# Reordering the first pass of a two-layer graph network with routed experts: the mean-square product ahead of the transposes, the scales ahead of an older block's places

## The chip, the cores and the metric

The kernel runs on one core of one Trainium2 chip. Its metric is the time of one launch on the device in microseconds (us); the time before is the median of three runs. Five engines work side by side, each through its own instructions in the order in which they were written: TensorE (PE in the profile, PEld for its weight loads), VectorE (DVE), ScalarE (ACT), GpSimd (POOL) and SyncE (SP). [...]

## The reference, cut to what matters

The input is 8192 tokens of 256 numbers, 64 to a graph. Two layers follow each other, each a graph part and a mixture of experts. Only the first half of layer 0 is touched here:

```python
xn  = layernorm(x)
agg = epsilon * xn + adj @ xn                     # per graph of 64 tokens
h   = agg @ W1 + b1                               # 256 -> 1024
h   = silu(h * rsqrt(mean(h * h) + 1e-6) * rms_w) # mean over the 1024
x1  = x + h @ W2 + b2                             # 1024 -> 256
xn1 = layernorm(x1)
logits = xn1 @ gate_w.T                           # 64 experts, the best 6 are taken
... the 6 experts' 256x256 matrices, weighted by the softmax of the 6 logits,
... then layer 1: another graph part and 8 experts, the best 2 taken
```

## The kernel before

TensorE works in fp32 here, but for the counting and bias products. The kernel goes through the program in stages: a first pass over 32 blocks of 256 tokens (the graph part of layer 0, and routing), pages of 128 rows through the 64 experts, a second pass over the 32 blocks, and pages through the 8 experts of layer 1. The routing sends each token's row six times to a table in HBM, to the place that its expert's counter gives; each of the 12 sends of a block is an indirect DMA that GpSimd issues.

The first pass is software-pipelined. Step `s` runs the stages below in this order, each for block `s - lag`; since each engine keeps the program's order, this list is also the order on every engine.

```python
staggered(NB, (
    (3, choose),                             # DVE: best 6 of the logits in pg
    (2, residual_a),                         # DVE: x1 = po + x, statistics
    (-2, load), (-1, norm_a),                # DVE: statistics of x
    (0, hidden 0), (0, hidden 1),            # PE: h; ACT: Square of each part
    (2, residual_s), (-1, norm_s),           # ACT: Ln, Exp of the variances
    (-1, norm_e), (3, weigh),                # DVE; ACT: Exp
    (0, hidden 2), (0, hidden 3),            # PE; ACT: Square
    (3, count),                              # PE: into the PSUM tile route
    (2, residual_b), (-1, norm_b),           # DVE; ACT: six copies of xn1 into xs
    (0, split_late),
    (1, project first tile, parts 0-3),      # PE
    (0, square_sum),                         # DVE: three adds
    (-1, aggregate),                         # PE; ACT: copy aggT <- ps
    (-1, load_late),
    (1, project first tile, parts 4-7),      # PE
    (2, turn),                               # PE: 4 transposes; ACT: copy xn1T <- ps
    (0, rms),                                # PE: 1 product; ACT: Ln, Exp, table load
    (3, place),                              # DVE: normalize, books, places; GpSimd: sends
    (1, project second tile),                # PE
    (2, gate),                               # PE: logits
    (0, scale),                              # DVE: 8 scales; ACT: 8 Silu, table load
    (1, load_lattice),
))
```

The stages that the change moves (cut):

```python
def hidden(b, j):                            # four tiles ph in PSUM for the four j
    B["ph", j] = ph = ph_pool.tile([P, 2, C], F32, name="ph")
    ...                                      # 4 products; then ACT:
    for c in range(2):
        nc.scalar.activation(sq[:, 2*j+c, :], ph[:, c, :], AF.Square, bias=..., scale=1.0)

def square_sum(b):                           # 8 parts -> 4 -> 2 -> 1
    h = KH
    while h > 1:
        h //= 2
        nc.vector.tensor_add(sq[:, :h, :], sq[:, :h, :], sq[:, h:2 * h, :])

def rms(b):
    nc.tensor.matmul(rms_b, lhsT=mean, rhs=sq[:, 0, :], start=True, stop=True)
    blocks[b]["rms"] = ops.rstd(rms_b, 1e-6, ...)          # ACT: Ln, then Exp
    nc.scalar.preload_act_table_set("silu_and_others")

def turn(b):
    pt = psum.tile([P, KD, C], F32, name="ps")             # pool ps: 2 buffers
    ops.transpose(pt, B["xs"][:, :, 0, :])
    nc.scalar.copy(xn1T, pt)

def scale(b):                                # reads ph, so it also frees ph
    for c in range(KH):
        nc.vector.scalar_tensor_tensor(hT[:, c, :], B["ph", c // 2][:, c % 2, :],
                                       b1[:, c:c + 1], B["rms"], op0=ALU.add, op1=ALU.mult)
        nc.scalar.activation(hT[:, c, :], hT[:, c, :], AF.Silu, scale=rms_w[:, c:c + 1])
    nc.scalar.preload_act_table_set("natural_log_exp_and_others")

def place(b):
    r0.normalize(*B["w"], B["xs"])                         # DVE: 3 small instructions
    r0.send(r0.places(b, B["hot"]), B["xs"])               # GpSimd: 12 indirect DMAs
    ...

def places(self, b, hot):                                  # of the router
    if self.J > 1 and b >= self.epoch and b % self.epoch < 3:     # epoch is 4
        (self.move_on, self.grow, self.note)[b % self.epoch]()    # DVE: 7, 10 or 6
    ...                                                    # DVE: 9 more, the last the rows
```

In three blocks of four, one of `move_on`, `grow` and `note` keeps the router's books: which expert needs a further stretch of the table.

Of the kernel before, what the change touches and what calls it, by code (L numbers as in the profile page):

```python
# [78 lines left out]
class Router:  # L79
# [199 lines left out]
    def normalize(self, w, den, xs):  # L279
# [2 lines left out]
        nc.vector.reciprocal(den, den)  # L282
        nc.vector.tensor_mul(xs[:, :, :, D + 1], w, den.unsqueeze(2).to_broadcast([P, T, K]))

    def places(self, b, hot):

        nc, T, E, K, n = self.nc, self.T, self.E, self.K, self.name
        if self.J > 1 and b >= self.epoch and b % self.epoch < 3:
            (self.move_on, self.grow, self.note)[b % self.epoch]()
        pos, cnt = self.psum[:, 0], self.psum[:, 1]  # L290
        run = self.run
        self.run = self.counts.tile([P, T, E], F32, name=n + "run")
        nc.vector.tensor_add(run[:, 1, :], run[:, 0, :], cnt[:, 0, :])
        nc.vector.tensor_add(self.run[:, 0, :], run[:, 1, :], cnt[:, 1, :])
        place = self.work.tile([P, T, E], F32, name=n + "place", bufs=1)
        nc.vector.tensor_add(place, pos, run)
        if self.J > 1:
            over = self.work.tile([P, T, E], F32, name=n + "over", bufs=1)
            nc.vector.tensor_tensor(over, place, self.end.unsqueeze(1).to_broadcast([P, T, E]), op=ALU.is_ge)
            nc.vector.tensor_mul(over, over, self.delta.unsqueeze(1).to_broadcast([P, T, E]))  # L300
            nc.vector.tensor_add(place, place, over)
        prod = self.work.tile([P, T, K, E], F32, name=n + "prod", bufs=1)
        nc.vector.tensor_mul(prod, hot, place.unsqueeze(2).to_broadcast([P, T, K, E]))
        row = self.small.tile([P, T, K], F32, name=n + "rowf")
        nc.vector.tensor_reduce(row, prod, op=ALU.add, axis=AX.X)
        out = self.small.tile([P, T, K], I32, name=n + "row")
        nc.vector.tensor_copy(out, row)
        return out
# [166 lines left out]
def two_layer_gnn_moe_kernel(ctx: ExitStack, tc: tile.TileContext, a: dict, out: bass.AP):  # L475
# [83 lines left out]
    r0 = Router(tc, const, small, dram, N, D, E0, K0, T, P, 14 * P, 4, "r0", 3)  # L559
# [23 lines left out]
    with tc.tile_pool(name="c0", bufs=1) as c0, \  # L583
# [9 lines left out]
        blocks = [dict() for _ in range(NB)]  # L593
# [96 lines left out]
        def project(b, t, lo, hi):  # L690
            B = blocks[b]
            if t == 0 and lo == 0:
                B["po"] = psum.tile([P, T, D], F32, name="ps")
                nc.tensor.matmul(B["po"], lhsT=r0.ones, rhs=late["L0_gnn_b2"], start=True, stop=False)
            for c in range(lo, hi):
                nc.tensor.matmul(B["po"][:, t, :], lhsT=B["hT"][:, c, ts(t, P)], rhs=w2[:, c, :],  # L696
                                 start=False, stop=(t == T - 1 and c == KH - 1))
# [44 lines left out]
        def count(b):  # L742
            r0.count(blocks[b]["hot"])

        def place(b):
            B = blocks[b]
            r0.normalize(*B["w"], B["xs"])
            r0.send(r0.places(b, B["hot"]), B["xs"])
            if b == READY - 1:
                r0.look_back()  # L750
            if b == 20:
                r0.look(EARLY)

        def load_lattice(b):
# [26 lines left out]
            (-1, aggregate),  # L781
            (-1, load_late),
            (1, lambda b: project(b, 0, 4, KH)),
            (2, turn),
            (0, rms),
            (3, place),
            (1, lambda b: project(b, 1, 0, KH)),
            (2, gate),
            (0, scale),
            (1, load_lattice),  # L790
        ))
        r0.page_table(sq.rearrange("p c n -> p (c n)"))
# [119 lines left out]
    with tc.tile_pool(name="c3", bufs=1, reuse_waits="tile") as c3, \  # L912
# [17 lines left out]
        blocks = [dict() for _ in range(NB)]  # L930
# [298 lines left out]
```

## Time and profile before

| | us |
|---|---|
| median of 3 runs | 2074.68 (2069.03 to 2075.51) |
| span of the profiled execution | 2434.4 |
| PE busy in it | 2043.7 (84%) |
| DVE busy | 1184.6 (49%) |
| POOL busy | 1144.3 (47%) |
| ACT busy | 1009.9 (41%) |

The profiled execution is longer than the timed ones. Its first pass lasts from the start to about 800 us; the transposes and products of the first expert pages follow from 806 us on. In a line of the timeline the columns are start and busy time in us, engine, source line, operation, operands, how many were merged, and, in brackets, how long the engine had been idle before it and who released it. TensorE's fp32 products appear as two records each, except for the transposes.

For reading the timeline: L663 is a product of `hidden` and L666 its Square, L673 `square_sum`, L677 the product of `rms`, L58 and L59 its Ln and Exp (and those of other stages), L76 the transposes of `turn` and L725 their copy, L656 the copy of `aggregate`, L685 the scales and L687 the Silu, L281 to L283 `normalize`, L226 to L259 the books, L293 to L307 `places`, L204 and L205 `choose`, L715 the six copies into `xs`, L314 the sends.

### The profile page before, as it was taken

The page shows a single profiled execution, that of the slowest core. Times are in us where ns is not written, and L with a number is a line of the kernel's source. Part 1 is how long each engine was busy: PE and PEld are TensorE (multiplying, and loading weights), DVE is VectorE, ACT ScalarE, POOL GpSimd, SP SyncE. Part 2 cuts the span into 40 slices and gives each one's busy share as a digit, 9 for nine tenths or more (in the row PEclk, how much of TensorE's full clock was granted, in tenths as well). Part 3 has the DMA queues.
Part 4 walks back from the last instruction along what each step waited for, and adds up shares of the span by engine and source line. Part 5 has one row for each costly group of instructions (what it writes and reads, how often), then busy time and mean ns, then how long its engine had stood idle before and what let it go on. Part 6 is the DMA issues. An engine that isn't in the chain of part 4 may idle for free. (4 is left out here: it accounts for less than half of the span.)

```text
span 2434.4 us, 36827 instructions
## 1 busy us (share of the span) xinstructions
PE 2043.7 (84%) x10516; PEld 1750.1 (72%) x10516; DVE 1184.6 (49%) x3981; ACT 1009.9 (41%) x2033; POOL 1144.3 (47%) x1134
## 2 busy tenths in 40 slices
PE   7887878878876578778787877888988899999997
PEld 6776767767665467666666765777777788888886
DVE  5677657667765622222222224777778422222221
ACT  5765656656655112111111212555555333333332
POOL 0345444554555656666666661233333444444443
PEclk9999889989898689889999888999999899999998
DMA  3223333433234678765555526887774476666665
GB/s 109 91 99 113 125 118 106 131 122 119 101 108 157 196 234 234 218 181 176 174 170 174 160 80 242 289 267 239 248 235 138 128 181 162 162 159 165 160 167 101
DMA packets 282557, 397.88 MB, mean 163 GB/s; under 512 B 56025, under 2 KB 236393, under 8 KB 282353
## 3 DMA queue, kind: packets, MB, share of 16 engines
q1 hardware_dynamic: 202880, 246.61, 34.5%
q0 software_dynamic: 64416, 136.14, 18.8%
q10 hardware_dynamic: 15056, 12.69, 1.6%
q8 instruction: 94, 1.54, 0.3%
q14 instruction: 111, 0.90, 0.1%
HBM read 222.84 MB, written 176.64 MB: 164 GB/s over the span
## 5 line engine op out<-in xcount | busy, mean ns | idle before, releaser
L314 POOL DMA_INDIRECT r0x<-xs,r0row x384 | 385.6, 1004 | 442.3 <-issue 343.3
L883 PE MATMUL py<-lat,pxT 128*128 x1616 | 427.9, 412 | 114.2 <-ACT pxT L870 86.0
L321 POOL DMA_INDIRECT r0y<-px x404 | 392.3, 971 | 230.9 <-DVE px L887 107.2
L883 PEld LDWEIGHTS py<-lat,pxT 128*128 128x128 f32 x1616 | 317.2, 207 | 169.7 <-ACT pxT L870 97.9
L887 DVE TENSOR_SCALAR px<-py,px 128x256 f32<-128x256 f32 x404 | 170.9, 478 | 453.2 <-PE py L883 160.9
L331 POOL DMA_INDIRECT out_x<-py_s,px x138 | 214.6, 1555 | 294.3 <-DMA out_x<-py_s,px 136.8
L870 ACT COPY pxT<-pt 128x512 f32<-128x512 f32 x202 | 113.9, 588 | 515.3 <-remote 161.9
L696 PE MATMUL ps<-lat 128*128 128x256 f32 x1024 | 267.2, 412 | 15.6 <-issue 14.4
L1167 ACT ACTIVATE phid<-ph,pw 128x256 f32<-128x256 f32 x276 | 130.9, 474 | 322.6 <-issue 211.3
L663 PE MATMUL ph<-lat 128*128 128x256 f32 x1024 | 243.8, 396 | 20.6 <-issue 14.3
L1165 PE MATMUL ph<-pxT,pw 128*128 128x256 f32 x1104 | 251.1, 381 | 0.7 <-ACT pxT L1156 0.7
L696 PEld LDWEIGHTS ps<-lat 128*128 128x128 f32 x1024 | 213.1, 211 | 53.5 <-issue 17.9
L1185 PE MATMUL py<-fw,phid 128*128 (+1 forms) x1104 | 249.7, 379 | 0.0
L663 PEld LDWEIGHTS ph<-lat 128*128 128x128 f32 x1024 | 201.1, 199 | 53.6 <-issue 19.4
L1165 PEld LDWEIGHTS ph<-pxT,pw 128*128 128x128 f32 x1104 | 210.7, 191 | 29.9 <-ACT pxT L1156 1.1
L1185 PEld LDWEIGHTS py<-fw,phid 128*128 128x128 f32 x1104 | 204.5, 190 | 25.0
L314 POOL DMA_INDIRECT r1x<-xs,r1row x128 | 126.2, 986 | 202.1 <-DVE bn_rs L1004 114.2
L666 ACT ACTIVATE lat<-ph,c_L_gnn_b 128x256 f32<-128x256 f32 x256 | 102.5, 471 | 113.1 <-remote 52.9
L868 PE MATMUL pt<-ident,px 128*128 128x128 f32 x808 | 132.3, 285 | 7.7 <-issue 7.6
L868 PEld LDWEIGHTS pt<-ident,px 128*128 128x128 f32 x808 | 107.7, 149 | 33.9 <-issue 14.0
L685 DVE SCALAR_TENSOR_TENSOR lat<-ph,c_L_gnn_b,rms 128x256 f32<-128x256 f32 x256 | 103.1, 475 | 52.3 <-ACT rms L59 45.7
L1188 DVE TENSOR_TENSOR py_s<-py,pb 128x512 f32<-128x512 f32 x69 | 47.8, 692 | 155.4 <-PE py L1185 155.4
(303 smaller groups left out, 2872.1 us busy)
## 6 DMA issues: line engine op xcount, KB each, us to landing
px<-r0x SPq DMA_DIRECT2D x404, 129.0 KB
y<-r0y SPq DMA_DIRECT2D x64, 768.0 KB
pw<-in_L_ffn_W1b SPq DMA_DIRECT2D x69, 514.0 KB
px<-r1x SPq DMA_DIRECT2D x69, 258.0 KB
x<-x SPq DMA_DIRECT2D x64, 256.0 KB
pb<-in_L_ffn_b SPq DMA_DIRECT2D x69, 128.0 KB
r0x<-r0filler ACTq DMA_DIRECT2D x64, 129.0 KB
lat<-in_x SPq DMA_DIRECT2D x32, 256.0 KB
```

What stands on the lines that cost most here:

```text
L314: i = self.nc.gpsimd.indirect_dma_start(out=self.table[:, :], out_offset=bass.IndirectOffsetOnAxis(ap=row[:, t, k:k + 1], axis=0), in_=xs[ ...
L321: d = self.nc.gpsimd.indirect_dma_start(out=self.answer[:, :], out_offset=bass.IndirectOffsetOnAxis(ap=x[:, self.D:self.D + 1].bitcast(I32 ...
L331: i, d = f"{self.name}add{i}", self.nc.gpsimd.indirect_dma_start(out=self.total[:, :], out_offset=bass.IndirectOffsetOnAxis(ap=x[:, self.D ...
L663: nc.tensor.matmul(ph[:, c, :], lhsT=w1[:, k, ts(2 * j + c, P)], rhs=B["aggT"][:, k, :], start=(k == 0), stop=(k == KD - 1))
L696: nc.tensor.matmul(B["po"][:, t, :], lhsT=B["hT"][:, c, ts(t, P)], rhs=w2[:, c, :], start=False, stop=(t == T - 1 and c == KH - 1))
L868: nc.tensor.transpose(pt[:, k, ts(q, P)], Q["px"][:, q, ts(k, P)], ident)
L870: nc.scalar.copy(xT[:, :, :n * P], pt[:, :, :n * P])
L883: nc.tensor.matmul(py[:, q, :], lhsT=xT[:, k, ts(q, P)], rhs=lat[:, ds(regs["e"][(2 * j + q) % 4], 1), k, :].rearrange("p o d -> p (o d)") ...
L887: nc.vector.tensor_scalar(px[:, q, :D], py[:, q, :], px[:, q, D + 1:D + 2], None, op0=ALU.mult)
L1165: nc.tensor.matmul(ph, lhsT=w[:, k * F1 + c * P:k * F1 + (c + 1) * P], rhs=Q["xT"][:, k, :], start=(k == 0), stop=(k == KD - 1))
L1167: nc.scalar.activation(hid[:, c, :], ph, AF.Relu, bias=w[:, KD * F1 + c:KD * F1 + c + 1], scale=1.0)
L1185: nc.tensor.matmul(py[:, t, :], lhsT=Q["hid"][:, c, ts(t, P)], rhs=fw2[:, ds(e, 1), c, :].rearrange("p o d -> p (o d)"), start=(c == 0), s ...
```

## The change

Three things are moved; nothing is added or taken out. The product of the mean squares (`rms`, with its Ln, Exp and table load) goes ahead of the transposes (`turn`, with its copy). `place` is split: its bookkeeping (`normalize` and the router's `books`) keeps its place ahead of the scales, and the rest (`places` and the sends) comes after them. The purpose is that the scales of the current block, which free the PSUM tiles of `hidden` and feed the Silu, need not stand behind the places of a block three steps older.

```diff
-    def places(self, b, hot):
-
-        nc, T, E, K, n = self.nc, self.T, self.E, self.K, self.name
+    def books(self, b):
+
         if self.J > 1 and b >= self.epoch and b % self.epoch < 3:
             (self.move_on, self.grow, self.note)[b % self.epoch]()
+
+    def places(self, b, hot):
+
+        nc, T, E, K, n = self.nc, self.T, self.E, self.K, self.name
         pos, cnt = self.psum[:, 0], self.psum[:, 1]
 ...
+        def books(b):
+            B = blocks[b]
+            r0.normalize(*B["w"], B["xs"])
+            r0.books(b)
+
         def place(b):
             B = blocks[b]
-            r0.normalize(*B["w"], B["xs"])
             r0.send(r0.places(b, B["hot"]), B["xs"])
 ...
             (1, lambda b: project(b, 0, 4, KH)),
+            (0, rms),
             (2, turn),
-            (0, rms),
+            (3, books),
+            (0, scale),
             (3, place),
             (1, lambda b: project(b, 1, 0, KH)),
             (2, gate),
-            (0, scale),
             (1, load_lattice),
```

## The prediction

> **What bounds the kernel now.** I read the page first. Its span is 2434.4 us, but the timed runs take 2074.68, so 360 us of this profile are not in the time that counts. The list of waits within the first pass (100 to 750 us, 26 or 27 steps) tells which idle time may belong to the tracing and which to the kernel:
>
> ```profile
> PE ps L76 <- ACT lat L656: 77.5, 23, 6.8
> ACT lat L656 <- remote: 58.5, 12, 6.0
> ACT lat L666 <- remote: 52.9, 12, 7.0
> DVE lat L685 <- ACT rms L59: 40.4, 9, 8.3
> DVE lat L673 <- issue: 15.7, 13, 5.0
> PE ph L663 <- DVE lat L685: 3.6, 6, 0.9
> ```
>
> ScalarE stands still some 5 us at a time (58.5 / 12), about once a step, at its copy of `aggregate` or at a Square, and no engine of this core is named. TensorE's waits at the transposes (77.5 us) and most of VectorE's waits for `rms` (up to 8.3 us) follow these stops. A step with such a stop takes 23.5 to 26.5 us. I choose to hold the stops for a cost of tracing: 26 x 5 to 7 us is 130 to 180 us, a plausible share of the missing 360. What a change does to them will then not show in the timed runs. So I work out the step from a stretch without a stop, the timelines of VectorE, ScalarE and TensorE between 514 and 536 us:
>
> ```profile
> 514.52 2.41 DVE L673 TENSOR_TENSOR lat<-lat 128x1024 f32<-128x1024 f32 x3 [0.82 <-ACT lat L666]
> 516.85 0.16 DVE L281 TENSOR_REDUCE r0den<-r0w 128x2 f32<-128x12 f32 x1
> 517.33 0.22 DVE L253 SCALAR_TENSOR_TENSOR r0cum<-r0alloc,r0cum 128x64 f32<-128x64 f32 x1
> 519.31 0.22 DVE L293 TENSOR_TENSOR r0run<-r0run,route 128x64 f32<-128x64 f32 x1
> 523.06 3.22 DVE L685 SCALAR_TENSOR_TENSOR lat<-ph,c_L_gnn_b,rms 128x256 f32<-128x256 f32 x8
> 526.21 0.23 DVE L204 MAX8 r0top<-rms_p 128x8 f32<-128x64 f32 x1
> 533.55 1.95 DVE L673 TENSOR_TENSOR lat<-lat 128x1024 f32<-128x1024 f32 x2 [0.91 <-issue]
> ```
>
> ```profile
> 518.83 0.59 ACT L725 COPY xn1T<-ps 128x512 f32<-128x512 f32 x1 [0.75 <-PE ps L76]
> 519.31 0.48 ACT L58 ACTIVATE rms<-rms_p,eps 128x256 f32<-128x256 f32 x1
> 519.82 0.42 ACT L59 ACTIVATE rms<-rms 128x256 f32<-128x256 f32 x1
> 520.25 1.28 ACT L679 ACT_TABLE_LOAD   x1
> 523.58 3.30 ACT L687 ACTIVATE lat<-lat,c_L_gnn_rms_weight 128x256 f32<-128x256 f32 x8 [2.04 <-DVE lat L685]
> 531.97 1.55 ACT L666 ACTIVATE lat<-ph,c_L_gnn_b 128x256 f32<-128x256 f32 x4
> 533.39 3.23 ACT L715 ACTIVATE xs<-x,bn_nm,rstd 128x1536 f32<-128x1536 f32 x2
> ```
>
> ```profile
> 518.19 0.60 PE L76 MATMUL ps<-ident,xs 128*128 128x128 f32 x4
> 518.62 0.60 PE L677 MATMUL rms_p<-lat,mean 128*128 128x256 f32 x2
> 523.99 7.17 PE L663 MATMUL ph<-lat 128*128 128x256 f32 x32 [0.47 <-DVE lat L685]
> ```
>
> The reader is to see that Exp ended at 520.24 and the scales began at 523.06: 2.8 us in which `rms` was ready and VectorE was still at the places; and that TensorE then waited 0.47 us at `hidden` for the first scales. That is what the change aims at. But VectorE was not idle in these 2.8 us. From start to start, in order, its step is: scales 3.15 (526.21 - 523.06); `choose` to the end of `norm_b` 6.42 (to 532.63); idle 0.92, as it waits for the last Squares; `square_sum` 2.33; `normalize` 0.48; books 1.98 (519.31 - 517.33, here `note`); places 3.75 (523.06 - 519.31). For the other blocks the same timeline has `grow` at 2.38 (287.44 to 289.82) and `move_on` at 1.45 (seven starts, 755.16 to 756.6). So VectorE's loop is 17.05 us plus 0, 1.45, 2.38, 1.98 of books: 17.05, 18.50, 19.43, 19.03, on the mean 18.50. TensorE's own step at full clock, start to start: hidden 7.0, count and bias 0.9, project 1.73, aggregate 0.89, project 1.73, transposes 0.44, rms 0.44, project 3.45, gate 0.84, together 17.4. As a check, the step of 16.46 us after 739.51, which has no aggregate, fits 17.4 - 0.9. So without stops VectorE's loop is the bound, by about 1 us a step, and TensorE's wait at `hidden` is how that shows.
>
> **What the Trainium skill says.** TensorE: Matmul & The Clock Gate, the table at its head: ScalarE, VectorE and GpSimd have a strict first-in first-out queue of 8. So an instruction that waits holds up all behind it, and only the order matters. The trace agrees: Silu waits 2.04 us behind scales that wait behind places. The same page, "What's actually happening": the clock goes to half after an idle window of about 3.4 us. The trace shows it: the mean clock is 0.86 to 0.93 in the first pass with its 5 us stops, and a timed run without the stops should have nearly full clock. ScalarE: Activation LUTs, "Table sets: the hidden batching unit": copy is in every set, so the copy of `turn` behind the load of the Silu set needs no further load; "What ACT_TABLE_LOAD costs": about 1283 ns for the load, and the trace has 1.28 us. It also adds 1380 ns of drain, which the trace doesn't show: Exp ends at 520.24 and the load starts at 520.25.
>
> **The change part by part.** No instruction is added or removed; I count from the start of the scales, X.
>
> VectorE: after the scales (3.15) now come the places (3.75), then `choose` to `norm_b` (6.42). All that hangs on them on ScalarE comes 3.75 us later. The idle 0.92 stays, since it is the way VectorE, variances on ScalarE, Squares, VectorE, all in order. `square_sum` thus starts at X + 14.24 and its result is there at X + 16.65 (2.41). Then two things run side by side. VectorE does normalize and books: X + 14.24 + 2.33 + 0.48 + books = X + 17.05, 18.50, 19.43 or 19.03. TensorE does the product: about 0.1 for the semaphore, 0.65 from its start to Ln (270.25 to 270.93 in another step), so X + 17.4. But ScalarE has not come so far: its last four Squares began at 531.97, 8.91 after X, now 12.66; then 1.42 to the copies into xs (533.39), 3.11 for those, 0.5 for the copy of `aggregate`: Ln at X + 17.69. Ln to Exp 0.51, Exp to scale 0.45: the next scales can't start before X + 18.65. So the loop becomes the larger of both: 18.65, 18.65, 19.43, 19.03, mean 18.94, where it was 17.05 (TensorE's 17.4 at best), 18.50, 19.43, 19.03. Before the change the places filled this time: `rms` was ready at about X + 16.4, before VectorE's 17.05.
>
> Over four steps that is + 1.25 to 1.6 + 0.15, or 0.35 to 0.44 a step. Books begin with block 4 at step 7, places end their share at step 31, so 25 to 28 steps: + 9 to 12 us. If the timed TensorE is slower than 17.4, it hides part of it; at 18.7 a step the difference is 0.25, + 7 us. What TensorE wins at `hidden` (0.47 to 0.86 us in a step without a stop) it will spend at `rms`, waiting for `square_sum`: off the path.
>
> The end of the pass: GpSimd's sends take 12 x (0.97 + 0.30) = 15.3 us a block, less than a step, so it has no backlog until the last step with scales (31). Block 28's places then end 3.2 us later (scales in front), and four blocks of sends, 61 us, follow one behind the other, because the steps after it are shorter than 15.3. The expert pages wait for the last send, so up to + 3.2 us, less if the page table ends later.
>
> The copy of `turn` comes 2.2 us later on ScalarE (0.51 + 0.43 + 1.28), but the second half of project, 3.45 us, lies before its reader: free.
>
> Sum: + 7 to 12 for the loop, 0 to 3 for the end, and some chance that I overrate VectorE's loop: + 7, or 2082 us.
>
> **The rivals.** First, TensorE is the bound and its wait at `hidden` is lost time: 25 x 0.5 to 0.85 us is 12 to 21 us to win, 2054 to 2062. For it: the wait is there in nearly all steps that no stop precedes, named with its releaser. Against it: TensorE's 17.4 is under VectorE's 18.5. Second, the stops are real in timed runs too. Then after each stop `rms` no longer stands behind the transposes, Ln starts about 2 us sooner (copy at 492.18, Ln at 494.82, against 492.8), and TensorE saves the 0.5 to 1.06 us of the product after the stop: about 10 to 20 us to win, 2055 to 2065. Against it: 2434 against 2075. Third, VectorE is faster untraced, below 17.4: then nothing but the end is left, 2075 to 2078. Fourth, the later sends hold up a buffer: `xs` has 3, a block's sends end about X + 6.9 + 15.3 + 2 = 24 and its buffer is written again after X + 33; no wait.
>
> **Range and chances.** My own path gives 2080 to 2090, the third 2075 to 2078, the first two about 2055 to 2065 with a fifth of the weight. So 2082, and 2062 to 2097 should hold it 8 times in 10. 2% are 41 us, 1.6 us in each of 26 steps; no path reaches that: faster 0.03, slower 0.03, same 0.94.
>
> **What would show it.** In the profile after: no waits of `hidden` for scales; a new wait of VectorE's scales for Exp (L59's place), 1 to 1.6 us in the steps without books, in steps without a stop; a wait of TensorE's `rms` for `square_sum`; Ln right behind the copy of `aggregate`. Where stops fall, the profile's span may even be shorter while the timed run is not. I am wrong if the timed run is more than 10 us faster: then VectorE's loop was not the bound. I am wrong upward beyond 20 us if a further table load or a wait of the sends shows.

## The result and the profile after

| | before | after |
|---|---|---|
| median | 2075.1 us (4 runs) | 2094.11 us (4 runs) |
| ratio | | 1.0098, 95% interval 1.0079 to 1.0117 |
| span of a profile | 2073.1 us | 2092.2 us |

The change costs 19 us. The page of before that the prediction read shows 2434 us; the profile of 2073.1 us is that of the run `control` below, the same program. All lines "of before" in this part are from it.

First the list of waits between 100 and 550 us, of before and then of after; the columns are who waited for whom, us in total, times, and the longest.

```profile
PE ps L76 <- ACT lat L656: 11.8, 16, 1.0
PE ph L663 <- DVE lat L685: 8.4, 12, 0.9
DVE lat L673 <- ACT lat L666: 22.7, 24, 1.2
```

```profile
PE rms_p L680 <- DVE r0den L281: 11.7, 19, 0.9
PE ps L76 <- ACT lat L659: 8.6, 23, 0.4
PE rms_p L680 <- DVE lat L676: 2.9, 5, 0.8
DVE lat L676 <- ACT lat L669: 22.1, 24, 1.0
DVE lat L688 <- ACT rms L59: 10.5, 7, 1.5
```

The stops of ScalarE that the prediction read are in neither. TensorE's 8.4 us at `hidden` are gone, as the change meant, and 14.6 us at `rms` are in their place (11.7 + 2.9; `r0den` is the small instruction right behind `square_sum`, which is what the product reads and so its true releaser). VectorE's wait for the last Squares is as before, some 0.92 us a step. The last line is the new one: VectorE's scales wait for Exp, 1.5 us in each of the 7 steps in which the router has no books to keep.

One such step, block 14, in the timelines of before. The upper four lines are VectorE's, the next three ScalarE's:

```profile
262.42 3.22 DVE L685 SCALAR_TENSOR_TENSOR lat<-ph,c_L_gnn_b,rms 128x256 f32<-128x256 f32 x8
...
272.91 2.41 DVE L673 TENSOR_TENSOR lat<-lat 128x1024 f32<-128x1024 f32 x3 [0.92 <-ACT lat L666]
275.71 0.21 DVE L293 TENSOR_TENSOR r0run<-r0run,route 128x64 f32<-128x64 f32 x1
279.46 0.87 DVE L685 SCALAR_TENSOR_TENSOR lat<-ph,c_L_gnn_b,rms 128x256 f32<-128x256 f32 x2
...
275.87 0.59 ACT L656 COPY lat<-ps 128x512 f32<-128x512 f32 x1
277.69 0.48 ACT L58 ACTIVATE rms<-rms_p,eps 128x256 f32<-128x256 f32 x1
278.20 0.42 ACT L59 ACTIVATE rms<-rms 128x256 f32<-128x256 f32 x1
```

and of after, with TensorE's product below:

```profile
281.55 2.41 DVE L676 TENSOR_TENSOR lat<-lat 128x1024 f32<-128x1024 f32 x3 [0.94 <-ACT lat L669]
284.27 0.18 DVE L283 TENSOR_TENSOR xs<-r0w,r0den 128x12 f32<-128x12 f32 x1
285.96 3.23 DVE L688 SCALAR_TENSOR_TENSOR lat<-ph,c_L_gnn_b,rms 128x256 f32<-128x256 f32 x8 [1.51 <-ACT rms L59]
289.10 0.21 DVE L296 TENSOR_TENSOR r0run<-r0run,route 128x64 f32<-128x64 f32 x1
...
284.51 0.59 ACT L659 COPY lat<-ps 128x512 f32<-128x512 f32 x1
284.97 0.50 ACT L58 ACTIVATE rms<-rms_p,eps 128x256 f32<-128x256 f32 x1
285.51 0.42 ACT L59 ACTIVATE rms<-rms 128x256 f32<-128x256 f32 x1
...
284.11 0.67 PE L680 MATMUL rms_p<-lat,mean 128*128 128x256 f32 x2 [0.77 <-DVE lat L676]
```

Before, from the start of `square_sum` to the scales, VectorE has 6.55 us of unbroken work (279.46 - 272.91), and Exp is done at 278.62, in its midst: nobody waits. After, `square_sum` and `normalize` end near 284.45, the places are no longer there to fill the time, and VectorE stands still until Exp ends at 285.93. The places follow at 289.10, in full. So the scales are 2.1 us nearer to `square_sum` (4.41 against 6.55), but VectorE's whole round is longer by this wait, and VectorE's round is what sets the step.

The length of a step, from one product of the mean squares to the next in TensorE's timeline, tells the same for all four kinds of block (one value of each kind, steps 18, 19, 16 and 17; the columns on the right are the experiments below):

| books of the block | before | after | `scales_alone` | `place_behind` | `half_places_2` | `books_early` |
|---|---|---|---|---|---|---|
| none | 17.35 | 18.62 | 20.00 | 19.11 | 18.00 | 17.36 |
| move_on | 18.25 | 18.66 | 20.00 | 20.59 | 17.39 | 17.35 |
| grow | 19.42 | 19.41 | 20.00 | 21.52 | 19.30 | 17.91 |
| note | 19.07 | 19.11 | 20.00 | 21.16 | 18.96 | 18.10 |
| first to last product, us | 564.4 | 579.6 | 610.0 | 621.3 | 562.4 | 545.1 |

Of the 19 us, 15.2 are thus in the loop, and the rest of the span, after the last product, went from 1482.4 to 1486.5 us: 4.1 at the end of the pass and behind it (the first product comes 0.2 us sooner).

### The profile page after: what moved, and what is told of

Read it like the earlier page. It is cut to its first block, busy times and chain, and to the rows that moved or that the text cites. A ratio compares the mean times of both kernels' runs of the same rounds, so it can differ in the third digit from the quotient of the medians.

```text
span 2092.2 us, 36857 instructions
## 1 busy us (share of the span) xinstructions
PE 1940.8 (93%) x10516; PEld 1673.9 (80%) x10516; DVE 1188.0 (57%) x3981; ACT 1015.1 (49%) x2033; POOL 1141.3 (55%) x1134
## 5 line engine op out<-in xcount | busy, mean ns | idle before, releaser
L317 POOL DMA_INDIRECT r0x<-xs,r0row x384 | 379.4, 988 | 292.9 <-issue 151.7
L891 PE MATMUL py<-lat,pxT 128*128 x1616 | 388.6, 384 | 17.9 <-ACT pxT L878 13.8
L895 DVE TENSOR_SCALAR px<-py,px 128x256 f32<-128x256 f32 x404 | 177.0, 480 | 309.9 <-PE py L891 306.2
L891 PEld LDWEIGHTS py<-lat,pxT 128*128 128x128 f32 x1616 | 293.5, 192 | 57.8 <-ACT pxT L878 17.9
L699 PE MATMUL ps<-lat 128*128 128x256 f32 x1024 | 237.7, 381 | 0.0
L666 PE MATMUL ph<-lat 128*128 128x256 f32 x1024 | 232.2, 386 | 2.7 <-DVE lat L688 2.0
L666 PEld LDWEIGHTS ph<-lat 128*128 128x128 f32 x1024 | 195.2, 193 | 29.4 <-issue 2.4
L699 PEld LDWEIGHTS ps<-lat 128*128 128x128 f32 x1024 | 190.9, 191 | 23.1
L317 POOL DMA_INDIRECT r1x<-xs,r1row x128 | 130.0, 1015 | 71.9 <-issue 22.7
L1187 DVE TENSOR_SCALAR p<-p 128x2 f32<-128x2 f32 x69 | 11.7, 169 | 226.7 <-ACT p L1186 226.7
L876 PEld LDWEIGHTS pt<-ident,px 128*128 128x128 f32 x808 | 101.2, 143 | 39.6 <-DMA px<-r0x 9.6
```

Of the source, the lines that this page charges most:

```text
L317: i = self.nc.gpsimd.indirect_dma_start(out=self.table[:, :], out_offset=bass.IndirectOffsetOnAxis(ap=row[:, t, k:k + 1], axis=0), in_=xs[ ...
L666: nc.tensor.matmul(ph[:, c, :], lhsT=w1[:, k, ts(2 * j + c, P)], rhs=B["aggT"][:, k, :], start=(k == 0), stop=(k == KD - 1))
L876: nc.tensor.transpose(pt[:, k, ts(q, P)], Q["px"][:, q, ts(k, P)], ident)
L891: nc.tensor.matmul(py[:, q, :], lhsT=xT[:, k, ts(q, P)], rhs=lat[:, ds(regs["e"][(2 * j + q) % 4], 1), k, :].rearrange("p o d -> p (o d)") ...
L895: nc.vector.tensor_scalar(px[:, q, :D], py[:, q, :], px[:, q, D + 1:D + 2], None, op0=ALU.mult)
```

## The experiments

The theory: VectorE's round sets the step in before; the change takes away the work that lay beside rms on its way through TensorE and ScalarE, so that in steps with few books a wait joins the round. The rivals: TensorE's new wait or the later copy of `turn`; the end of the pass (later sends); any delay of what comes behind the scales.

**The same program again.** No edit.

> The kernel before, with nothing changed, for a profile that holds no stops of ScalarE. VectorE's loop as the bound: 2072 to 2078 us; steps of the first pass 17.4 (no books), 18.5 (move_on), 19.4 (grow) and 19.0 us (note), with TensorE waiting at hidden for the scales and no wait of VectorE's scales for Exp. TensorE as the bound (rival): 17.4 to 17.9 in all four kinds of step. If the stops are there again in a profile whose time is near 2075, they belong to the kernel and my reading of them was wrong.

2075.11 us, ratio 1.0002 (0.9992 to 1.0013). The steps are 17.35, 18.25, 19.42 and 19.07, and scales start 17.04 us after the last ones in a step without books (262.42 to 279.46), where the sum was 17.05. VectorE's round is the bound in before.

**The product alone ahead of the transposes.**

```diff
-            (2, turn),
             (0, rms),
+            (2, turn),
```

> Only the product of the mean squares goes ahead of the transposes; places stay whole and ahead of the scales. VectorE's loop as the bound: rms was ready before the places ended and is only ready earlier now, so nothing changes: within 3 us of before. If the rival holds and the loss of the change lies in TensorE's new wait at rms or in the later copy of turn, this kernel shows the loss: 2085 to 2095.

2077.04 us, ratio 1.0005 (0.9994 to 1.0015); first to last product 564.4 us as before. This half of the change costs nothing by itself, and neither does the later copy of `turn`, which is in it too.

**The scales alone ahead of the places.**

```diff
             (2, turn),
             (0, rms),
-            (3, place),
+            (3, books), (0, scale), (3, place),
 ...
-            (0, scale),
```

> Only the scales go ahead of the places (books in front); the product stays behind the transposes. My theory, the way through ScalarE's queue: Ln now stands behind the copies into xs, the copy of aggregate, the transposes and the copy of turn, at X + 12.66 + 4.53 + 1.83 = X + 19.0, and the scales at X + 20.0 in every kind of step (19.4 and 19.0 before at most, 18.9 on the mean in the changed kernel): 25 to 28 us more than the changed kernel, some 2115 to 2122. Rival, that only the end of the pass (later sends) costs: the same as the changed kernel, 2092 to 2096.

2125.26 us, ratio 1.0239 (1.0222 to 1.0256), 3 us over the range. From step 3 on nearly every step takes 20.0 us, whatever the books (the longest is 20.9). ScalarE's queue in one of these steps:

```profile
313.26 3.23 ACT L718 ACTIVATE xs<-x,bn_nm,rstd 128x1536 f32<-128x1536 f32 x2
316.38 0.59 ACT L659 COPY lat<-ps 128x512 f32<-128x512 f32 x1
317.72 0.59 ACT L728 COPY xn1T<-ps 128x512 f32<-128x512 f32 x1 [0.75 <-PE ps L76]
318.20 0.48 ACT L58 ACTIVATE rms<-rms_p,eps 128x256 f32<-128x256 f32 x1
318.71 0.42 ACT L59 ACTIVATE rms<-rms 128x256 f32<-128x256 f32 x1
```

Ln stands behind the copy of `turn`, which waits for the transposes, which wait for the buffer that the copy of `aggregate` frees. So it begins at 318.20, though `square_sum` had ended at 315.83 (313.42 + 2.41). With the scales in front, the product has to go ahead of the transposes too: that half wins back 31 us (2125 to 2094).

**All of place behind the scales, the books too.**

```diff
-            (3, books),
             (0, scale),
+            (3, books),
             (3, place),
```

> The changed kernel with the whole of place behind the scales, normalize and the books too. If what counts is that nothing of VectorE's work lies beside the wait for rms, the 0.48 us of normalize and the books (0, 1.45, 2.38, 1.98) are added in full: steps of 19.1, 20.6, 21.5, 21.1 us against 18.65, 18.66, 19.4, 19.05 in the changed kernel; 10 x 0.5 + 6 x (1.9 + 2.1 + 2.1) = 41 us, and about 2 at the end: 2132 to 2140. Rival, that the books are hidden behind other work anyway: within 5 us of the changed kernel, 2090 to 2098.

2137.89 us, ratio 1.0296 (1.0273 to 1.0318); the steps 19.1, 20.6, 21.5 and 21.2 are the expected ones. What stands behind the scales is added in full, since VectorE now waits for Exp in every step:

```profile
301.37 3.23 DVE L688 SCALAR_TENSOR_TENSOR lat<-ph,c_L_gnn_b,rms 128x256 f32<-128x256 f32 x8 [2.00 <-ACT rms L59]
304.51 0.15 DVE L281 TENSOR_REDUCE r0den<-r0w 128x2 f32<-128x12 f32 x1
...
320.51 3.23 DVE L688 SCALAR_TENSOR_TENSOR lat<-ph,c_L_gnn_b,rms 128x256 f32<-128x256 f32 x8 [2.00 <-ACT rms L59]
```

Keeping the books in front was worth 44 us to the change.

**The old order in steps without books.** The scales stay behind the places where no books would cover rms, and in all steps before 7.

```diff
-            (0, scale),
+            (0, lambda b: scale(b) if b >= 7 and (b - 3) % 4 < 3 else None),
             (3, place),
+            (0, lambda b: None if b >= 7 and (b - 3) % 4 < 3 else scale(b)),
```

> The changed kernel, but in the steps without books (and all before step 7) the scales stay behind the places, so that no wait of VectorE for Exp is left. My sum says that the loop's loss sits in the steps whose books are too short to cover rms: the loop comes back to that of before (35.6 us for the pair of steps without books and with move_on, as before), and only the end of the pass, some 4 us, is left: 2077 to 2082. If the loss were TensorE's wait at rms or the later copy of turn, in all steps alike, a third of it would go: 2086 to 2090.

2084.35 us, ratio 1.0042 (1.0025 to 1.0059): outside both ranges, half of the loss. First to last product takes 569.8 us, 5.4 more than before; the steps are 18.0, 18.4, 19.4 and 19.1. The end of the pass takes its share too: the last send comes 70.5 us behind the last product of the mean squares, in before 67.0. In the loop a changed step after an old one doesn't return as much as I had reckoned. TensorE and VectorE around step 18, which is in the old order, and step 19, with move_on, in the new:

```profile
352.81 0.67 PE L680 MATMUL rms_p<-lat,mean 128*128 128x256 f32 x2 [0.72 <-DVE r0den L281]
353.83 0.66 PE L76 MATMUL ps<-ident,xs 128*128 128x128 f32 x4 [0.35 <-ACT lat L659]
370.81 0.59 PE L680 MATMUL rms_p<-lat,mean 128*128 128x256 f32 x2
...
372.39 3.23 DVE L688 SCALAR_TENSOR_TENSOR lat<-ph,c_L_gnn_b,rms 128x256 f32<-128x256 f32 x8 [0.71 <-ACT rms L59]
```

In step 18 TensorE waits 0.72 us for `square_sum` and then 0.35 for the copy of `aggregate`; the rest of its round is without a gap, and its next product comes after 18.0 us, where 17.35 would do. So Ln and Exp of step 19 come late, and its scales wait for them, 0.71 us here and 0.7 to 0.8 in most such steps. Here TensorE's lateness does reach VectorE.

**Half of the places back in front.** The six instructions up to the place of each row (1.7 us) go with the books; product with `hot`, sum, cast and sends stay behind the scales.

```diff
 def books(b):
     ...
     r0.normalize(*B["w"], B["xs"])
     r0.books(b)
+    B["place"] = r0.places(b, B["hot"])      # the first six instructions
 def place(b):
-    r0.send(r0.places(b, B["hot"]), B["xs"])
+    r0.send(r0.rows(B["hot"], B["place"]), B["xs"])
```

> The changed kernel with the first six instructions of places (1.7 us, up to the place of each row) back ahead of the scales with the books; only the product with hot, the sum and the cast (2.06 us) and the sends stay behind. If the loss is only that VectorE has too little to do while rms is made, it is covered now: VectorE is busy 2.33 + 0.48 + 1.69 = 4.5 us after square_sum begins, before rms is ready at 4.1, and ScalarE reaches Ln 1.7 us sooner. The steps come back to 17.4, 18.2, 19.4, 19.05 as before; with a little at the end 2074 to 2080. Rival, that any work behind the scales delays the Squares and so the loop: half of the loss stays, 2084 to 2087.

2452.52 us where before took 2438.39 on the same chip, ratio 1.007 (1.0039 to 1.0101). On this chip the kernel before takes 17% longer, with stops as in the page that the prediction read. What part of the 14 us is the change's stays open, as the changed kernel was not timed there. The second trial is on a chip on which before takes 2075.7 us:

> The same kernel as half_places, which ran on a chip on which the kernel before takes 2438 us; again on another. As there: if the loss is only that VectorE has too little to do while rms is made, 2074 to 2080 where before takes 2075; rival, that any work behind the scales delays the loop, 2084 to 2087. If before takes some 2438 again, only the ratio counts: 1.000 to 1.003 or 1.005 and more.

2074.9 us, ratio 0.9994 (0.9983 to 1.0005). The loss is gone, though 2.06 us of work and the sends still stand behind the scales. The list of waits between 100 and 550 us:

```profile
PE rms_p L685 <- DVE r0den L281: 7.9, 11, 0.9
PE rms_p L685 <- DVE lat L681: 0.8, 1, 0.8
DVE lat L681 <- ACT lat L674: 23.3, 25, 1.0
DVE lat L693 <- ACT rms L59: 0.7, 2, 0.4
```

VectorE's wait for Exp fell from 10.5 us to 0.7, while TensorE still waits 8.7 us at `rms` (14.6 in the change). The loop is even 2.0 us shorter than in before (562.4 against 564.4), which makes up for a later end: the last send comes 70.5 us behind the last product of the mean squares, in before 67.0. So the loss of the loop was VectorE's uncovered wait. In this order neither the position behind the scales nor TensorE's wait costs the loop anything; where TensorE's lateness passes on to Exp, as in `bookless_old`, it does.

**The end of the pass, two trials.** First the last step with scales alone in the old order (`scale` for block 31 behind `place`).

> The changed kernel, but in the last step with scales (block 31) they stay behind the places, as before. If the end of the pass costs what the profiles show (places of block 28 end 8.7 us after the last rms instead of 4.5, and the sends follow), 3 to 5 us are won: 2089 to 2091. If the loop alone is the loss: 2094.

2095.26 us, ratio 1.0102 (1.0078 to 1.0126): nothing won. GpSimd's timeline shows why. In the lines below, of before and of after, each is the first send behind a gap of over 1 us near the end:

```profile
577.56 0.97 POOL L314 DMA_INDIRECT r0x<-xs,r0row  x1 [1.12 <-issue]
580.62 0.96 POOL L314 DMA_INDIRECT r0x<-xs,r0row  x1 [2.09 <-issue]
595.93 0.97 POOL L314 DMA_INDIRECT r0x<-xs,r0row  x1 [1.12 <-issue]
```

```profile
597.80 0.96 POOL L317 DMA_INDIRECT r0x<-xs,r0row  x1 [3.68 <-ACT lat L669]
600.86 0.96 POOL L317 DMA_INDIRECT r0x<-xs,r0row  x1 [2.10 <-issue]
```

Before, GpSimd is idle once more at 595.93, as the places of block 28 come; after, it has no such gap from those of block 27 on (597.80; the gap of 2.1 behind the first send of block 27 is in both), and five blocks of sends follow one another. Those places end 8.7 us ahead of the last product of the mean squares, in before 13.9 us ahead. So the old order has to begin earlier:

```diff
+            (0, lambda b: scale(b) if b < 27 else None),
             (3, place),
+            (0, lambda b: None if b < 27 else scale(b)),
```

> The changed kernel with the old order in the steps from block 27 on. In the profiles GpSimd sends without a gap from the places of block 27 on, not of block 28: these end 8.7 us ahead of the last rms in the changed kernel and 13.9 ahead of it in the one before. If this is what the end of the pass costs, 3 to 5 us are won: 2089 to 2091. If not, 2094 again, and the 4 us lie elsewhere.

2490.15 us on the slower chip, where before took 2438.39: ratio 1.0211 (1.0147 to 1.0274).

> The same kernel as old_from_27, again on another chip. If GpSimd's chain of sends from block 27 on is what the end of the pass costs, 2089 to 2091 where before takes 2075; if not, 2094.

2090.29 us, ratio 1.0073 (1.0047 to 1.0099), in the expected range, with first to last product at 579.4 us as in the change. The last sends, of before, of after, and of this kernel:

```profile
657.69 0.97 POOL L314 DMA_INDIRECT r0x<-xs,r0row  x1 [0.30 <-issue]
678.34 0.97 POOL L317 DMA_INDIRECT r0x<-xs,r0row  x1 [0.30 <-issue]
673.86 0.97 POOL L317 DMA_INDIRECT r0x<-xs,r0row  x1 [0.30 <-issue]
```

They start 67.0, 72.6 and 67.3 us behind the last product of the mean squares (73.1 in `last_step_old`). So in the traces the chain of sends ends 5.6 us later in the change, and this order takes that back. What follows the last send takes 1412 to 1419 us in all profiles without the stops, so a share of about 4 us is as close as single profiles tell; the intervals of the two ratios overlap.

**Books where VectorE idles.** The order of before, with `normalize` and the books ahead of `square_sum`:

```diff
+            (3, books),
             (0, square_sum),
 ...
             (0, rms),
             (3, place),                      # places and sends only
```

> The order of before, but normalize and the books stand ahead of square_sum, where VectorE idles 0.92 us a step for the last Squares. VectorE's loop as the bound: it falls by 0.48 us (no books) to 0.92, so 17.4 (TensorE), 17.6, 18.5, 18.1 against 17.4, 18.5, 19.4, 19.0: 0.7 a step on the mean, 16 to 19 us over the pass: 2056 to 2060. TensorE as the bound: within 3 us of before.

2051.41 us, ratio 0.9884 (0.9867 to 0.99): faster than both kernels, by 24 and 43 us. VectorE, at the start of a step with move_on:

```profile
282.81 0.73 DVE L648 TENSOR_SCALAR lat<-lat,bn_mv,rstd 128x256 f32<-128x256 f32 x2
283.46 0.16 DVE L281 TENSOR_REDUCE r0den<-r0w 128x2 f32<-128x12 f32 x1
...
285.38 2.40 DVE L676 TENSOR_TENSOR lat<-lat 128x1024 f32<-128x1024 f32 x3
287.70 0.21 DVE L296 TENSOR_TENSOR r0run<-r0run,route 128x64 f32<-128x64 f32 x1
```

The list of waits between 100 and 550 us has this line where before has 22.7 us:

```profile
DVE lat L676 <- ACT lat L669: 3.3, 7, 0.7
```

The idle 0.92 us in front of `square_sum` is filled, and the places still cover rms: VectorE's scales have no wait for Exp there. Two of four steps now take TensorE's own 17.36 us. The loop gives 19.3 us (564.4 to 545.1), as expected; the other 5 lie after the last product and were not expected. Of these, 2.2 are in the chain of sends (its last one starts 64.8 us behind the last product), and the rest is within what the profiles differ by after the last send.

**The books spread.** As the last, with note kept for the fourth block of each four instead of the third.

> The order with normalize and the books ahead of square_sum, with note moved from the third to the fourth block of each four, so that the two longest books don't follow each other. VectorE's mean step there (16.1 + 1.45 = 17.6) is only 0.2 over TensorE's 17.36, and 1.25 us are lost per four steps; spread, 0.9 or less: 2 to 5 us under 2051.4, so 2046 to 2050. If it doesn't pay: 2050 to 2053.

2052.86 us, ratio 0.9888 (0.9871 to 0.9906): no gain over `books_early`. Its steps are 17.4 (none), 17.8 (move_on), 18.2 (grow) and 17.4 us (note); the mean is the same 17.7, and first to last product is 543.9 us, 1.2 less. VectorE's sum over the four blocks counts here, hardly its order.

## Why the prediction was right in direction and short in size

**What bounds the kernel** held: VectorE's round of 17.05, 18.50, 19.43, 19.03 us is the bound, and the first rival, TensorE's wait at `hidden` as lost time, fell. That wait vanished and the kernel got slower. The third, a VectorE that is faster in the timed runs, fell too: its round without books took 17.04 us in `control`, where 17.05 was foreseen.

**The new round** held to a few hundredths: 18.65, 18.65, 19.43, 19.03 foreseen, and 18.62, 18.66, 19.41, 19.11 measured. Ln right behind the copy of `aggregate` is there (284.51, 284.97), and TensorE's new wait at `rms` is off the path, as `half_places_2` shows.

**The sum for the loop** was the term that was too small: 9 to 12 us, 15.2 measured. Steps 7 to 30 give 10.4 us, within it (0.43 a step, where 0.35 to 0.44 was foreseen). But the count of 25 steps begins with the books, at step 7, and that of 28 gives three steps before them only the mean of a step. The places begin at step 3, and the steps 3 to 6, whose blocks have no books, lose most: 0.97 + 1.29 + 1.32 + 1.31 = 4.9 us. The lower end, 0.35, also took TensorE's 17.4 as a floor under VectorE's round; it is none, as the next step gives the time back (17.35 + 18.25 = 35.6 in the steps of before, 17.05 + 18.50 in VectorE's sum), so the upper end was the right one.

**The end of the pass** was put at 0 to 3.2 us, from block 28 on. About 4 fell there or behind it, and the sends run without a gap from block 27 on. Steps without books, such as block 27's, lost more, and so the chain starts a block earlier than foreseen.

**The stops** were read wrongly. They are not a cost of tracing: the profile of `control` has none, and there is a chip on which the timed runs of the kernel before take 2438 us and the profile of `half_places` has them again. Their absence from the times to be predicted was right for a reason that was not the one given, which is luck. TensorE's clock went with the stops, as foreseen: its mean is 1.00 between 100 and 550 us in `control` and 0.87 between 100 and 750 us in `half_places`. Such means show a lower clock and not by how much it falls at a time; in the page of before eight products of `project` take 3.57 us at 511.22, behind a stop, and 1.89 at 531.88. The second rival, a gain where the stops are, wasn't seen there either: `old_from_27`, which has the changed order for 27 of 32 blocks, is 1.021 times as long there. VectorE's scales now wait for Exp behind the stops, 167.1 us between 100 and 750 us, where the page of before had 40.4:

```profile
DVE lat L688 <- ACT rms L59: 167.1, 22, 9.1
```

**The number.** 2094 lies within the stated 2062 to 2097, but above the 2080 to 2090 of the prediction's own path. For giving the rivals weight I went down from that path's sum to + 7; without that discount, and with the steps 3 to 6 at what they lost, it would have been about 14 to 19.

**What was to show it** showed: no wait at `hidden`, a wait for Exp of 1.5 us in steps without books (1 to 1.6 foreseen), one at `rms` for `square_sum`. No further table load shows: the two loads of a step appear 32 times each in before and after.

## What to carry to other kernels

An engine that is busy 90% of the time can be the bound while another is busy 96% (VectorE 405.7 and TensorE 429.8 of 450 us in before): add up its round, idle waits that are part of the round included, and compare sums over a whole period. An instruction that seems to stand in the way of the critical result may be what covers that result's own way through other engines; before it is moved, look for what will lie beside the wait, and move work into the idle time that is already there instead. When a pipelined loop is counted, count its first rounds too, which may lack the very work that would hide the wait.

## What the runs showed of the hardware

One chip differed by 17% from three others on one program: 2438 us for the kernel before, and 2075 to 2076 on the three. On the slower one ScalarE stops for up to 7.6 us some once a step, with no engine of the core as the releaser, and TensorE's mean clock over the whole run is 0.92 instead of 0.97. VectorE has such waits too. From the list of waits of `half_places` there, 100 to 750 us:

```profile
ACT lat L664 <- remote: 107.0, 19, 7.6
DVE r0run L296 <- remote: 33.2, 10, 4.8
PE ps L76 <- ACT lat L664: 78.4, 18, 8.1
```

What stops them stays open; no run here was made to find it.
